# PixArt block on one core: banks of the maxima, place of a normalisation, and the order of loads in the start-up

## The chip, the cores and the metric

The kernel runs on one core of a Trainium2 chip. The metric is the device time of one execution in microseconds (us); three runs of the kernel before gave 813.94, 815.04 and 817.46 us, so its median is 815.04 us. A separate execution was profiled.

Engines: PE is TensorE (matrix products; PEld is its weight load, which runs ahead of it), DVE is VectorE, ACT is ScalarE, POOL is GpSimd, SP issues transfers (DMA). [...]

## What is computed

```python
x_norm = modulate(_ln(x), shift_a, scale_a)
q, k, v = split(x_norm @ W_qkv + b_qkv)           # 16 heads of 16
x = x + gate_a * ((softmax(q @ k.T * scale) @ v) @ W_proj + b_proj)
q_c = _ln(x) @ W_qc + b_qc;  k_c, v_c = split(_ln(context) @ W_kvc + b_kvc)
x = x + (softmax(q_c @ k_c.T * scale) @ v_c) @ W_cproj + b_cproj
h = gelu(modulate(_ln(x), shift_m, scale_m) @ W_mlp1 + b_mlp1) @ W_mlp2 + b_mlp2
x = x + gate_m * h
```

There are 16 batches of 256 tokens and 256 channels, in fp32. Shift, scale and gate come from `silu(cond_1024) @ W_mod + b_mod`.

## The kernel before, in words

**Units.** The work is 32 attention units: a self-attention (s) and a cross-attention (c) for each batch. Their order is s0 s1 s2 s3, then s4 c0 s5 c1 ... s15 c11, then c12 to c15. So from unit 4 to unit 27 the even units are s and the odd ones c. The MLP of all batches follows; some of its first steps lie in the last units.

**Beats.** One unit takes eight beats (`beat(n, k)`, line 944, k = 0 to 7; n is the unit whose softmax is being worked on, and n = -1 is a run of eight beats ahead of unit 0). A beat opens with `visit(n, k)` (line 929):

- `s_tile` (line 589) computes a tile of scores for the *next* unit, n+1, tokens in rows: four matmuls `s<-big` into the two banks of the PSUM tile `sp` (named s in the profile). One DVE instruction (`TENSOR_REDUCE mx<-s`, 128x1024) then takes the row maxima of both banks. The next beat's four matmuls may start only when it has ended, since they write the same two banks.
- `t_part` (line 624) computes the scores of the *current* unit with keys in rows, into the two banks of `st`; ACT takes their exponential (`pt<-st`). The maxima have become a row of the query tile before that.

After the visit a beat has pieces of other units: "lanes" (24 matmuls that run the projections of two units side by side), a transposition, or the product of exponentials and values, `av_part` (line 654, tile o).

**Around the change.** In beats 0 and 4 PE runs, after the visit, `m_part` (line 614, a transposition of the maxima, tile psm) and two `av_part` (32 matmuls into one bank, tile o). In beat 2, `turn(1)` of the previous unit (line 535) transposes the second half of its attention output into a bank (tile psA), and, where unit n+3 is s, its normalised x is transposed into another bank (psT_s), with the high part of the split by ACT (xTh_s) and the low part by DVE (xTl_s, 128x256 twice, in beat 3). `norm(1)` (line 542) of the previous unit reads psA on DVE: a reciprocal (rc) and a product (A). Before, it stands in beat 3 behind xTl_s. In beat 6, `turn(0)` transposes the first half for the current unit; if unit n+3 is c, a second transposition (psT_q) stands in that beat too.

**PSUM banks.** `sp` and `st` own two banks each. The other four are two tags of two banks: LONG ("gen", the lanes) and SHORT ("tr": psm, o, psT, psA and others). A SHORT tile gets the bank of the two that comes free first; it waits until the last reader of the tile before is done.

**Order.** Every engine runs its instructions in the order in which they are written (`InOrder`, line 40). The start-up is written as a list of words in `E_` (line 55). `PRE` is the list ahead of the first beat, `SL` the words behind a beat (n, k). Words that matter here: `ld2`, `ld3`, `ld4` load x of units 2 to 4 (SP); `one0` to `one2` write rows of ones into the three key tiles (SP); `z..` are the memsets of these tiles (POOL); `L2a L2b L2c` are the layernorm of unit 2 (statistics and variance on DVE, then power and application on POOL); `T2t T2h T2l` its transposition, high part (ACT) and low part (DVE), `T2p` the low part by ACT and POOL; `K2a K2m` its key projection (12 matmuls); `V0`, `V1` the value projections of units 0 and 1; `M0` an `m_part`; `b5`, `c4`, `d3` and so on are filler matmuls (4, 5, 3 ...) into sp, st or a SHORT bank; `vone` writes ones on POOL; `rest` takes the next step of `setup_rest` (line 221): first the loads for the attention's gate and bias rows (four weight or modulation tiles and bias rows; issued by ACT's queue before), then three small products ps_ga, ps_pb, ps_cb with DVE behind them, then three weight loads, then splits of weights on POOL.

Of the kernel before, what the change touches and what calls it, by code (L numbers as in the profile page):

```python
# [21 lines left out]
def pixart_block(  # L22
# [8 lines left out]
    B, N, H = x.shape  # L31
# [20 lines left out]
                return tc.keep_in_program_order(i) if self.on else i  # L52
            return issue

    E_ = {'M': ((-17, -12, -10, -1, 1), (0, 3, 4, 7, 9), (8, 11, 13, 15)), 'CUT': 8, 'LN': {'s': 'pool', 'c': 'pool', 'q': 'pool'}, 'ON': (1, 1, 1), 'L0': -16, 'L1': 1, 'S0': -7, 'A0': 0, 'T0': 1, 'H': (7, 11, 14, 15), 'S1': 5, 'A1': 7, 'L2': 9, 'T1': 9, 'S2': 32, 'AP': 23, 'DV': (0, 1), 'HP': (1, 0), 'BZ': {}, 'AV': {1: [(1, 2), (1, 3)], 9: [(0, 0), (0, 1)]}, 'AHEAD': (0, 0, 0, 0, 0, 2), 'W1P': [(-9, 1), (-8, 1), (-7, 1), (-6, 1), (-5, 1), (-5, 5), (-4, 1), (-4, 3), (-4, 5), (-3, 1), (-3, 3), (-3, 5), (-2, 1)], 'W2P': [(-4, 7), (-3, 0), (-3, 4), (-3, 6), (-3, 7), (-2, 2), (-2, 4), (-2, 6), (-1, 0), (-1, 1)], 'XP': 1, 'IL': 1, 'MF': 0, 'SH': 4, 'RAMP': 1, 'HA': 1, 'MP': 16, 'W': (7, 1, 0, 0), 'PRE': 'z0qp z0kp load silu b12 brow L0a turn L0b b4 L0d scale T0t sc1 hik lok T0h T0l b4 shift b4 hiq L1a L1b bk loq K0a K0b K0x0 K0x1 K0y0p K0y1p L1d T1t K0l T1h K0l0 K0l1 Q0a Q0m bq Q0h Q0x0 Q0y0p Q0x1 Q0y1p T1l Q0l Q0l0 Q0l1 ld2 z1kp z1qp K1a K1b hiv lov Q1a Q1b K1x0 K1x1 K1y0 K1y1 K1l K1l0 K1l1 Q1x0 Q1x1 Q1y0 Q1y1 Q1l Q1l0 Q1l1 V0a V0b bv b5 rest vone ld3 z2kp z2qp', 'SL': {(-1, 0): 'one0 c4', (-1, 1): 'ld4 L2a V1a', (-1, 2): 'L2b L2c V1b', (-1, 3): 'rest one1', (-1,4): 'M0 rest', (-1, 5): 'T2t T2h T2l rest', (-1, 6): 'L3a K2a c1', (-1, 7): 'K2m L3b L3p L3c c3 one2 rest', (0, 0): 'd4', (0, 1): 'rest', (0, 2): 'd3', (0, 4): 'rest', (1, 0): 'rest', (1, 2): 'rest', (1, 4): 'rest', (30, 0): 'd3', (30, 1): 'd2', (30, 2): 'd3', (30, 5): 'd3', (31, 1): 'd2'}}

    PE = InOrder(nc.tensor, True)
    ACT, DVE, POOL, SP = (InOrder(e, True) for e in (nc.scalar, nc.vector, nc.gpsimd, nc.sync))
# [162 lines left out]
    def setup_rest():  # L221
        gb = work.tile([B, 2, 2, H], F32, tag="pt", name="gb", bufs=5)
        gA, bb = gb[:, 0], gb[:, 1]
        bc = const.tile([1, H], F32, name="bc")
        wg, wp = stage(W_mod, 2 * H, "wga", "g", 3, q=ACT), stage(W_proj, 0, "wp_f", "g", 3, q=ACT)
        ACT.dma_start(bb[:, 0], b_mod[2 * H:3 * H].partition_broadcast(B))
        ACT.dma_start(bb[:, 1], b_proj.partition_broadcast(B))
        ACT.dma_start(bc, b_cproj.partition_broadcast(1))
        wcp = stage(W_cproj, 0, "wcp_f", "x1", 5, q=ACT)
        yield  # L230
        pst = ps_gen("ps_ga")
        for k in range(KC):
            PE.matmul(pst[:B, :H], sT[:, k], wg[:, k], start=(k == 0), stop=(k == KC - 1))
        DVE.tensor_tensor(gA[:, 0], pst[:B, :H], bb[:, 0], ALU.add)
        yield
        pst = ps_gen("ps_pb")
        for k in range(KC):
            PE.matmul(pst[:B, :H], bqkv[:, 4 + k], wp[:, k], start=(k == 0), stop=(k == KC - 1))
        DVE.tensor_tensor(gA[:, 1], pst[:B, :H], bb[:, 1], ALU.add)
        DVE.tensor_tensor(gA[:, 1], gA[:, 1], gA[:, 0], ALU.mult)  # L240
        SP.dma_start(gd[:, 0:2], gA)
# [12 lines left out]
        yield  # L254
        split(Wkc[0], Wkc[1], wkc)
        yield
        split(Wqc[0], Wqc[1], wqc)
        yield
        split(Wvc[0], Wvc[1], wvc)
        yield  # L260
        split(Wcp[0], Wcp[1], wcp)
# [324 lines left out]

    turn_of_s = [0]

    def s_tile(u, g, par, t, bank=None):


        alone = bank is None
        if alone:
            turn_of_s[0] ^= 1
            bank = turn_of_s[0]
        for j in range(2):
            PE.matmul(sp[:, bank, j * N:(j + 1) * N],
                      u.q[par * 64:par * 64 + 63, 2 * g + j, t * P:(t + 1) * P],
                      u.k[par * 64:par * 64 + 63, 2 * g + j, :], start=True, stop=True)
            if j == 0:  # L600
                yield
        if u.mx is None:
            u.mx = work.tile([P, 2, 2, 4, NT], F32, tag="mx", name=f"mx_{u.n}", bufs=3)
        mx = u.mx.rearrange("p f r a t -> p r f a t")
        a = slice(2 * (g % 2), 2 * (g % 2) + 2)
        if alone:
            DVE.tensor_reduce(mx[:, par, g // 2, a, t], sp[:, bank].rearrange("p (j n) -> p j n", j=2),
                              AX.X, ALU.max)
        elif bank == 1:
            DVE.tensor_reduce(mx[:, :, g // 2, a, t], sp.rearrange("p r (j n) -> p r j n", j=2),  # L610
                              AX.X, ALU.max)
        yield

# [63 lines left out]
    for n, (kind, b) in enumerate(seq):  # L677
        u = Box()
# [247 lines left out]
    def unit(n):  # L926
        return units[n] if 0 <= n < nu else None

    def visit(n, k):


        v, e = unit(n + 1), k
        s = []
        if v:
            s = [s_tile(v, e // 2, par, e % 2, par) for par in range(2)]
        if n < 0:
            in_turn(*s)
            return
        t = [t_part(units[n], k, par) for par in range(2)]
        in_turn(*s)  # L940
        in_turn(*t)
        later.append(lambda: exp(units[n], k))

    def beat(n, k):
        if n < 0:
            visit(n, k)
            return
        cur, prev, nxt = unit(n), unit(n - 1), unit(n + 1)
        q2, q3, q4 = (v if v and v.n >= m else None
# [20 lines left out]
            q2.Q.send_high()  # L970
        if k == 6 and q2:
            q2.V.keep()
        visit(n, k)
        if k == 0:
            if cur:
                m_part(cur, 1)
# [21 lines left out]
        elif k == 2:  # L998
# [3 lines left out]
            if q3T:  # L1002
                q3T.T[0].turn()
                q3T.T[0].high()
            if p2 and p2.hurry:
                p2.add()
        elif k == 3:
            exps()
            if q3T and q3T.kind == "s":
                q3T.T[0].low()  # L1010
            if prev:
                p1.norm(1)
            run(lanes(q2 and q2.V, q2 and q2.Q))
            if q3T and q3T.kind == "c":
                q3T.T[0].low()
        elif k == 4:
            if nxt:
                m_part(nxt, 0)
            exps()
            if cur:  # L1020
                av_part(cur, 0)
                av_part(cur, 1)
            if prev:
                p1.aT.turn()
                p1.aT.high()
            if q2:
                q2.Q.low()
                q2.Q.send_low()
            if p3:
                p3.store()  # L1030
            if late:
                for f in lx.ln[1].steps:
                    f()
            if ls and not late:
                ls.ln[0].steps[0]()
                ls.ln[0].steps[1](False)
        elif k == 5:
# [12 lines left out]
            v = unit(n + 5)  # L1050
            if v and v.kind == "c":
                load(v)
        elif k == 6:
            exps()
            if cur:
                cur.post.begin()
                cur.post.turn(0)
            if lx:
                lx.T[1].turn()
                lx.T[1].high()  # L1060
            if early:
                early.ln[1].steps[1]()
                early.ln[1].steps[2]()
            if prev and whole:
                p1.proj(0)
                p1.proj(1)
        elif k == 7:
            exps()
            run(lanes(None if whole else p1, q3 and q3.K))
            if prev and whole:  # L1070
                p1.end()
                p1.add()
                p1.store()
            if cur:
                cur.post.norm(0)
            if lx:
                lx.T[1].low()
# [97 lines left out]
```

## Time and profile before

| | |
|---|---|
| three runs | 813.94, 815.04, 817.46 us |
| the profiled execution | 815.38 us, of which the span from the first to the last instruction is 813.6 us |
| granted PE clock | 1.000 |
| PE busy, 100 to 500 us | 96.3 to 97.6 of each 100 us |
| DVE busy, 100 to 500 us | 81.8 to 83.8 of each 100 us |
| ACT busy, 100 to 500 us | 80.9 to 83.0 of each 100 us |
| POOL busy, 100 to 500 us | 54.3 to 59.9 of each 100 us |
| first score tile (beat 0 ahead of unit 0) | PE at 25.01 us |
| first beat of unit 0 | PE at 40.52 us |
| last product o | PEld at 617.6 us |

How to read the rows of the timeline: start in us, duration in us, engine, line, operation, tile written, tiles read, shapes, count; in square brackets the time for which the engine sat idle before it, and what ended that. Almost everything has line 51, which records every call, so rows are told apart by tile.

### The profile page before, as it was taken

The page shows a single profiled execution, that of the slowest core. Times are in us where ns is not written, and L with a number is a line of the kernel's source. Part 1 is how long each engine was busy: PE and PEld are TensorE (multiplying, and loading weights), DVE is VectorE, ACT ScalarE, POOL GpSimd, SP SyncE. Part 2 cuts the span into 40 slices and gives each one's busy share as a digit, 9 for nine tenths or more (in the row PEclk, how much of TensorE's full clock was granted, in tenths as well). Part 3 has the DMA queues.
Part 4 walks back from the last instruction along what each step waited for, and adds up shares of the span by engine and source line. Part 5 has one row for each costly group of instructions (what it writes and reads, how often), then busy time and mean ns, then how long its engine had stood idle before and what let it go on. Part 6 is the DMA issues. An engine that isn't in the chain of part 4 may idle for free.

```text
span 813.6 us, 23717 instructions
## 1 busy us (share of the span) xinstructions
PE 780.9 (96%) x9461; PEld 658.9 (81%) x9461; DVE 597.9 (73%) x1050; ACT 585.2 (72%) x1022; POOL 464.6 (57%) x404
## 2 busy tenths in 40 slices
PE   9899999999999999999999999999889999999997
PEld 8687877777787877877778788777668999999997
DVE  4787878788888878878887888776663566566562
ACT  3277877878787888878788788877656665666663
POOL 5555737475563647546364767554436666666653
PEclk9999999999999999999999999999999999999999
DMA  4753444335353444534444454534311313212211
GB/s 147 190 156 104 131 117 122 102 110 151 90 143 107 132 119 111 152 90 137 112 133 120 139 151 118 147 106 128 96 41 41 91 41 78 79 43 75 79 40 53
DMA packets 89938, 87.88 MB, mean 108 GB/s; under 512 B 9506, under 2 KB 85572, under 8 KB 89828
## 3 DMA queue, kind: packets, MB, share of 16 engines
q1 hardware_dynamic: 88482, 84.76, 37.3%
q8 instruction: 75, 1.23, 0.7%
q10 hardware_dynamic: 1154, 1.08, 0.5%
q0 software_dynamic: 192, 0.52, 0.2%
q14 instruction: 35, 0.29, 0.1%
HBM read 26.97 MB, written 8.46 MB: 44 GB/s over the span
## 4 chain that ended last, share of the span: by engine, by line
PE 69%; DVE 16%; issue 5%; POOL 4%; DMA 1%; ACT 0%; SPq 0%; POOLq 0%
PE s L51 15%; PE o L51 13%; DVE mx L51 12%; PE ph L51 11%; PE st L51 9%; PE ps_q L51 3%; PE ps_kc L51 3%; PE ps_k L51 3%; PE ps_P_s L51 2%; PE ps_qc L51 2%; PE ps_v_s L51 1%; PE ps_P_c L51 1%; DVE xTl_s L51 1%; PE psm L51 1%; PE psT_m L51 1%
## 5 line engine op out<-in xcount | busy, mean ns | idle before, releaser
L51 DVE TENSOR_REDUCE mx<-s 128x4 f32<-128x1024 f32 x256 | 313.3, 1224 | 103.2 <-PE s L51 98.1
L51 ACT ACTIVATE pt<-st 128x1024 f32<-128x1024 f32 x256 | 261.2, 1020 | 46.8 <-PE st L51 39.7
L51 PE MATMUL s<-big 63*128 63x256 f32 x1024 | 121.4, 309 | 15.8 <-DVE mx L51 13.5
L51 PE MATMUL o<-pt,v 128*32 128x256 f32 x2048 | 123.8, 382 | 3.1 <-DVE A_s L51 3.1
L51 PEld LDWEIGHTS s<-big 63*128 63x128 f32 x1024 | 80.5, 185 | 52.3 <-DVE mx L51 32.3
L51 POOL TENSOR_TENSOR hl<-hf,hh 128x512 fp32r<-128x512 f32 x64 | 89.0, 1399 | 55.5 <-ACT hh L51 54.4
L51 PE MATMUL st<-big 64*128 64x256 f32 x1024 | 107.1, 281 | 1.8 <-ACT pt L51 1.8
L51 PEld LDWEIGHTS o<-pt,v 128*32 128x32 f32 x2048 | 60.0, 109 | 45.0 <-DVE A_s L51 5.7
L51 PEld LDWEIGHTS st<-big 64*128 64x128 f32 x1024 | 82.0, 186 | 3.6 <-ACT pt L51 2.2
L51 ACT ACTIVATE hf<-ph,bT 128x256 f32<-128x256 f32 x120 | 50.6, 475 | 28.1 <-PE ph L51 28.1
L51 ACT COPY oT<-o 128x512 f32<-128x512 f32 x63 | 37.0, 587 | 46.0 <-PE o L51 46.0
L51 ACT ACTIVATE hh<-ph,bT 128x256 fp32r<-128x256 f32 x120 | 50.5, 471 | 24.6 <-PE s L51 12.8
L51 POOL TENSOR_TENSOR xTl_as<-y_as,xTh_as 128x512 fp32r<-128x512 f32 x16 | 20.4, 1272 | 62.9 <-ACT y_as L51 62.9
L51 POOL TENSOR_TENSOR xTl_c<-y_c,xTh_c 128x512 fp32r<-128x512 f32 x16 | 20.7, 1292 | 61.3 <-PE s L51 52.8
L51 PE MATMUL ph<-wqch,wself 128*128 128x256 f32 x256 | 51.8, 285 | 0.0
L51 PE MATMUL ph<-wkch,wself 128*128 128x256 f32 x256 | 51.7, 285 | 0.0
L51 POOL TENSOR_TENSOR xTl_ac<-y_ac,xTh_ac 128x512 fp32r<-128x512 f32 x16 | 20.5, 1279 | 53.0 <-ACT y_ac L51 49.1
L51 PE MATMUL s<-big,hh 128*128 128x256 f32 x256 | 47.4, 282 | 0.0
L51 PE MATMUL st<-big,hh 128*128 128x256 f32 x256 | 47.2, 281 | 0.0
L51 DVE TENSOR_SCALAR xn_m<-x,mv_m,rs_m 128x256 f32<-128x256 f32 x32 | 38.2, 1233 | 10.8 <-POOL rs_m L51 10.8
L51 PEld LDWEIGHTS ph<-wqch,wself 128*128 128x128 f32 x256 | 42.0, 191 | 0.4 <-issue 0.4
L51 PEld LDWEIGHTS ph<-wkch,wself 128*128 128x128 f32 x256 | 41.9, 191 | 0.4
(221 smaller groups left out, 2375.1 us busy)
## 6 DMA issues: line engine op xcount, KB each, us to landing
big<-h_kc SPq DMA_DIRECT2D x64, 128.0 KB
big<-h_qc SPq DMA_DIRECT2D x64, 128.0 KB
big<-h_k SPq DMA_DIRECT2D x62, 128.0 KB
big<-h_q SPq DMA_DIRECT2D x62, 128.0 KB
big<-l_k SPq DMA_DIRECT2D x32, 128.0 KB
big<-l_q SPq DMA_DIRECT2D x32, 128.0 KB
c<-in_ctx_dram SPq DMA_DIRECT2D x16, 256.0 KB
g<-gd SPq DMA_DIRECT2D x16, 256.0 KB
```

Source lines behind the costliest of these rows:

```text
L51: i = f(*a, **k)
```

## The change

Four things are changed. In the eight beats ahead of unit 0 the score tiles go to `st` and `sp` in turn (k even: st, k odd: sp). In "light" beats (k = 6, unit n+3 not c, n from 4 to 27, which leaves n = 5, 7, ..., 23) the two halves of a score tile go to bank 0 of sp and to a SHORT bank, each with a DVE maximum of its own (128x512). `norm(1)` moves from beat 3 to beat 2. The words of the start-up are reordered: the first step of `rest` stands right behind `load` and is issued by SP, with x of unit 2 and `one0` behind it; the layernorm of unit 2 stands ahead of the first beat; its transposition stands in beat 1 with its low part on POOL; fillers are dropped or changed.

```diff
-'PRE': 'z0qp z0kp load silu ... Q0l Q0l0 Q0l1 ld2 z1kp z1qp K1a ... Q1l Q1l0 Q1l1 V0a V0b bv b5 rest vone ld3 z2kp z2qp'
+'PRE': 'z0qp z0kp load rest ld2 one0 silu ... Q0l Q0l0 Q0l1 z1kp z1qp K1a ... Q1l Q1l0 Q1l1 L2a L2b L2c V0a V0b bv b5 ld3'
-'SL': {(-1, 0): 'one0 c4', (-1, 1): 'ld4 L2a V1a', (-1, 2): 'L2b L2c V1b', (-1, 3): 'rest one1', (-1,4): 'M0 rest',
-  (-1, 5): 'T2t T2h T2l rest', (-1, 6): 'L3a K2a c1', (-1, 7): 'K2m L3b L3p L3c c3 one2 rest', (0, 0): 'd4', ...
+'SL': {(-1, 0): 'V1a', (-1, 1): 'T2t T2h T2p vone z2kp z2qp', (-1, 2): 'V1b', (-1, 3): 'rest', (-1,4): 'M0 rest one1 ld4',
+  (-1, 5): 'K2a L3a', (-1, 6): 'K2m L3b L3p L3c', (-1, 7): 'd3 one2 rest', (0, 0): 'd6 rest', ...
@@ setup_rest
-        wg, wp = stage(W_mod, 2 * H, "wga", "g", 3, q=ACT), stage(W_proj, 0, "wp_f", "g", 3, q=ACT)
-        ACT.dma_start(bb[:, 0], b_mod[2 * H:3 * H].partition_broadcast(B))
...
+        wg, wp = stage(W_mod, 2 * H, "wga", "g", 3), stage(W_proj, 0, "wp_f", "g", 3)
+        SP.dma_start(bb[:, 0], b_mod[2 * H:3 * H].partition_broadcast(B))
...
@@ s_tile
-    def s_tile(u, g, par, t, bank=None):
+    def s_tile(u, g, par, t, bank=None, home=sp):
+        apart = isinstance(home, tuple)
         for j in range(2):
-            PE.matmul(sp[:, bank, j * N:(j + 1) * N],
+            PE.matmul((home[bank] if apart else home[:, bank])[:, j * N:(j + 1) * N],
...
-        if alone:
-            DVE.tensor_reduce(mx[:, par, g // 2, a, t], sp[:, bank].rearrange("p (j n) -> p j n", j=2),
+        if alone or apart:
+            src = home[bank] if apart else sp[:, bank]
+            DVE.tensor_reduce(mx[:, par, g // 2, a, t], src.rearrange("p (j n) -> p j n", j=2),
                               AX.X, ALU.max)
         elif bank == 1:
-            DVE.tensor_reduce(mx[:, :, g // 2, a, t], sp.rearrange("p r (j n) -> p r j n", j=2),
+            DVE.tensor_reduce(mx[:, :, g // 2, a, t], home.rearrange("p r (j n) -> p r j n", j=2),
@@ beat
         if n < 0:
-            visit(n, k)
+            visit(n, k, (st, sp)[k % 2])
...
-        visit(n, k)
+        light = k == 6 and nxt and 3 < n < nu - 4 and not lx
+        visit(n, k, (sp[:, 0], ps_gen("s1", SHORT)) if light else sp)
@@ beat, k == 2
+            if prev:
+                p1.norm(1)
             if p2 and p2.hurry:
                 p2.add()
@@ beat, k == 3
-            if prev:
-                p1.norm(1)
             run(lanes(q2 and q2.V, q2 and q2.Q))
```

`visit` hands its new argument `home` to `s_tile`.

More of the change, by code (lines that the diff above doesn't have):

```diff
@@ L53, in __getattr__ @@
             return issue
-    E_ = {'M': ((-17, -12, -10, -1, 1), (0, 3, 4, 7, 9), (8, 11, 13, 15)), 'CUT': 8, 'LN': {'s': 'pool', 'c': 'pool', 'q': 'pool'}, 'ON': (1, 1, 1), 'L0': -16, 'L1': 1, 'S0': -7, 'A0': 0, 'T0': 1, 'H': (7, 11, 14, 15), 'S1': 5, 'A1': 7, 'L2': 9, 'T1': 9, 'S2': 32, 'AP': 23, 'DV': (0, 1), 'HP': (1, 0), 'BZ': {}, 'AV': {1: [(1, 2), (1, 3)], 9: [(0, 0), (0, 1)]}, 'AHEAD': (0, 0, 0, 0, 0, 2), 'W1P': [(-9, 1), (-8, 1), (-7, 1), (-6, 1), (-5, 1), (-5, 5), (-4, 1), (-4, 3), (-4, 5), (-3, 1), (-3, 3), (-3, 5), (-2, 1)], 'W2P': [(-4, 7), (-3, 0), (-3, 4), (-3, 6), (-3, 7), (-2, 2), (-2, 4), (-2, 6), (-1, 0), (-1, 1)], 'XP': 1, 'IL': 1, 'MF': 0, 'SH': 4, 'RAMP': 1, 'HA': 1, 'MP': 16, 'W': (7, 1, 0, 0), 'PRE': 'z0qp z0kp load silu b12 brow L0a turn L0b b4 L0d scale T0t sc1 hik lok T0h T0l b4 shift b4 hiq L1a L1b bk loq K0a K0b K0x0 K0x1 K0y0p K0y1p L1d T1t K0l T1h K0l0 K0l1 Q0a Q0m bq Q0h Q0x0 Q0y0p Q0x1 Q0y1p T1l Q0l Q0l0 Q0l1 ld2 z1kp z1qp K1a K1b hiv lov Q1a Q1b K1x0 K1x1 K1y0 K1y1 K1l K1l0 K1l1 Q1x0 Q1x1 Q1y0 Q1y1 Q1l Q1l0 Q1l1 V0a V0b bv b5 rest vone ld3 z2kp z2qp', 'SL': {(-1, 0): 'one0 c4', (-1, 1): 'ld4 L2a V1a', (-1, 2): 'L2b L2c V1b', (-1, 3): 'rest one1', (-1,4): 'M0 rest', (-1, 5): 'T2t T2h T2l rest', (-1, 6): 'L3a K2a c1', (-1, 7): 'K2m L3b L3p L3c c3 one2 rest', (0, 0): 'd4', (0, 1): 'rest', (0, 2): 'd3', (0, 4): 'rest', (1, 0): 'rest', (1, 2): 'rest', (1, 4): 'rest', (30, 0): 'd3', (30, 1): 'd2', (30, 2): 'd3', (30, 5): 'd3', (31, 1): 'd2'}}
@@ new lines, in pixart_block @@
+    E_ = {'M': ((-17, -12, -10, -1, 1), (0, 3, 4, 7, 9), (8, 11, 13, 15)), 'CUT': 8, 'LN': {'s': 'pool', 'c': 'pool', 'q': 'pool'}, 'ON': (1, 1, 1), 'L0': -16, 'L1': 1, 'S0': -7, 'A0': 0, 'T0': 1, 'H': (7, 11, 14, 15), 'S1': 5, 'A1': 7, 'L2': 9, 'T1': 9, 'S2': 32, 'AP': 23, 'DV': (0, 1), 'HP': (1, 0), 'BZ': {}, 'AV': {1: [(1, 2), (1, 3)], 9: [(0, 0), (0, 1)]}, 'AHEAD': (0, 0, 0, 0, 0, 2), 'W1P': [(-9, 1), (-8, 1), (-7, 1), (-6, 1), (-5, 1), (-5, 5), (-4, 1), (-4, 3), (-4, 5), (-3, 1), (-3, 3), (-3, 5), (-2, 1)], 'W2P': [(-4, 7), (-3, 0), (-3, 4), (-3, 6), (-3, 7), (-2, 2), (-2, 4), (-2, 6), (-1, 0), (-1, 1)], 'XP': 1, 'IL': 1, 'MF': 0, 'SH': 4, 'RAMP': 1, 'HA': 1, 'MP': 16, 'W': (7, 1, 0, 0), 'PRE': 'z0qp z0kp load rest ld2 one0 silu b12 brow L0a turn L0b b4 L0d scale T0t sc1 hik lok T0h T0l b4 shift b4 hiq L1a L1b bk loq K0a K0b K0x0 K0x1 K0y0p K0y1p L1d T1t K0l T1h K0l0 K0l1 Q0a Q0m bq Q0h Q0x0 Q0y0p Q0x1 Q0y1p T1l Q0l Q0l0 Q0l1 z1kp z1qp K1a K1b hiv lov Q1a Q1b K1x0 K1x1 K1y0 K1y1 K1l K1l0 K1l1 Q1x0 Q1x1 Q1y0 Q1y1 Q1l Q1l0 Q1l1 L2a L2b L2c V0a V0b bv b5 ld3', 'SL': {(-1, 0): 'V1a', (-1, 1): 'T2t T2h T2p vone z2kp z2qp', (-1, 2): 'V1b', (-1, 3): 'rest', (-1,4): 'M0 rest one1 ld4', (-1, 5): 'K2a L3a', (-1, 6): 'K2m L3b L3p L3c', (-1, 7): 'd3 one2 rest', (0, 0): 'd6 rest', (0, 1): 'rest', (0, 2): 'd3', (0, 4): 'rest', (1, 0): 'rest', (1, 2): 'rest', (1, 4): 'rest', (30, 0): 'd3', (30, 1): 'd2', (30, 2): 'd3', (30, 5): 'd3', (31, 1): 'd2'}}
@@ L224, in setup_rest @@
         bc = const.tile([1, H], F32, name="bc")
-        wg, wp = stage(W_mod, 2 * H, "wga", "g", 3, q=ACT), stage(W_proj, 0, "wp_f", "g", 3, q=ACT)
-        ACT.dma_start(bb[:, 0], b_mod[2 * H:3 * H].partition_broadcast(B))
-        ACT.dma_start(bb[:, 1], b_proj.partition_broadcast(B))
-        ACT.dma_start(bc, b_cproj.partition_broadcast(1))
-        wcp = stage(W_cproj, 0, "wcp_f", "x1", 5, q=ACT)
+        wg, wp = stage(W_mod, 2 * H, "wga", "g", 3), stage(W_proj, 0, "wp_f", "g", 3)
+        SP.dma_start(bb[:, 0], b_mod[2 * H:3 * H].partition_broadcast(B))
+        SP.dma_start(bb[:, 1], b_proj.partition_broadcast(B))
+        SP.dma_start(bc, b_cproj.partition_broadcast(1))
+        wcp = stage(W_cproj, 0, "wcp_f", "x1", 5)
         yield
@@ L927, in unit, with visit @@
         return units[n] if 0 <= n < nu else None
-    def visit(n, k):
+    def visit(n, k, home=sp):
         v, e = unit(n + 1), k
@@ L934, in visit @@
         if v:
-            s = [s_tile(v, e // 2, par, e % 2, par) for par in range(2)]
+            s = [s_tile(v, e // 2, par, e % 2, par, home) for par in range(2)]
         if n < 0:
```

## The prediction

> **What bounds the kernel now.** I read the chain of work that ended last first, by engine:
>
> ```profile
> PE 69%; DVE 16%; issue 5%; POOL 4%; DMA 1%; ACT 0%; SPq 0%; POOLq 0%
> ```
>
> PE carries the path, and DVE's 16% of 813.6 us (130 us) are places where PE stands and waits for DVE. The list of waits says where (total us, times, longest):
>
> ```profile
> PEld s L51 <- DVE mx L51: 32.3, 70, 1.3
> ...
> PEld o L51 <- DVE A_s L51: 5.7, 12, 0.5
> ```
>
> So 32.3 us of idle weight load lie ahead of a score tile that waits for the maxima of the tile before, and 5.7 us ahead of a product o that waits for the normalised A. The change works on both. The timeline then gives the size of each. From 60 to 500 us it repeats every two units (35.2 us: o at 209.18 and again at 244.48), so one pair speaks for all.
>
> **Normalisation a beat sooner.** First an odd unit: DVE in beats 3 and 4, PE's weight load in beat 4; then the same loads in an even unit.
>
> ```profile
> 241.80 1.23 DVE L51 TENSOR_REDUCE mx<-s 128x4 f32<-128x1024 f32 x1 [0.60 <-PE s L51]
> 242.94 0.87 DVE L51 SCALAR_TENSOR_TENSOR xTl_s<-psT_s,sc,xTh_s 128x256 fp32r<-128x256 f32 x2
> 243.72 0.25 DVE L51 RECIPROCAL rc_s<-psA_s 128x16 f32<-128x16 f32 x1
> 244.00 0.42 DVE L51 TENSOR_TENSOR A_s<-psA_s,rc_s 128x256 f32<-128x256 f32 x1
> ```
>
> ```profile
> 243.36 0.33 PEld L51 LDWEIGHTS st<-big 64*128 64x128 f32 x4
> 243.92 0.09 PEld L51 LDWEIGHTS psm<-ident,mx 128*16 128x16 f32 x1 [0.23 <-PE st L51]
> 244.48 1.45 PEld L51 LDWEIGHTS o<-pt,v 128*32 128x32 f32 x32 [0.47 <-DVE A_s L51]
> ```
>
> ```profile
> 261.16 0.33 PEld L51 LDWEIGHTS st<-big 64*128 64x128 f32 x4
> 261.63 0.09 PEld L51 LDWEIGHTS psm<-ident,mx 128*16 128x16 f32 x1
> 261.84 1.45 PEld L51 LDWEIGHTS o<-pt,v 128*32 128x32 f32 x32
> ```
>
> Psm and o need the two SHORT banks that psA and psT_s hold. In the odd unit psm takes psT_s's when xTl_s ends (243.81), and o must wait for A (244.42). In the even unit nothing waits: psm follows st by 0.47 us, o follows psm by 0.21. With the pair in beat 2, psA's bank is free two microseconds before psm, and o takes psT_s's bank. In the written-out order of the changed kernel, psm indeed no longer waits for DVE, and o waits for xTl_s. Then psm starts at 243.36 + 0.47 = 243.83 and o at 244.04 instead of 244.48: 0.44 us. What is late next is xTl_s: 243.81 and a hand-over of some 0.1, so 0.12 before o needs it. All twelve cases (units 1, 3, ..., 23) show the same 0.23 and 0.47, so 12 x 0.44 = **5.3 us**. Upper end: psm right at the end of st's loads (243.69), 0.56 x 12 = 6.7. Lower end: psm still behind xTl_s and o 0.21 behind it, 0.35 x 12 = 4.2.
>
> The pair is not free, it is hidden. Between two maxima DVE has, in beat 2, an idle 0.60 us (the bracket of 241.80; the same 0.60 stands at 259.60 in the even unit). The pair takes 0.28 to the next start and 0.34 more, 0.62 in all, against 0.69 from where the maximum of beat 2 lets go (239.97 + 1.14) to 241.80. It reads psA, whose transposition ends at 240.76 (PE, 240.10 + 0.66), before DVE is free at 241.11. Queued behind it on DVE is the maximum of beat 3, which ends at 243.03; the score tile that waits for it loads at 243.13. So there is 0.1 us to spare, in each of 31 units. Without that cover the price is up to 0.62 x 31 = 19 us.
>
> Does the 0.44 reach the end? Behind o comes beat 5. ACT idled 1.01 us there until o ended, DVE idled 1.14 until the score tile came, so both move with PE. The transfers of unit n+2's queries do not: SP issues the last at 248.06 to 249.34, bytes move until about 250.7 (the DMA view), and the tile that reads them loads at 252.7. Two microseconds remain for 0.6 us of shift.
>
> **Light beats.** Beat 6 of the odd unit, PE's loads, then DVE and ACT:
>
> ```profile
> 249.51 0.42 PEld L51 LDWEIGHTS psA_c<-ident,oT 128*128 128x128 f32 x4
> 250.66 0.30 PEld L51 LDWEIGHTS s<-big 63*128 63x128 f32 x4 [0.73 <-DVE mx L51]
> 250.89 0.31 PEld L51 LDWEIGHTS st<-big 64*128 64x128 f32 x4
> ```
>
> ```profile
> 249.39 1.23 DVE L51 TENSOR_REDUCE mx<-s 128x4 f32<-128x1024 f32 x1
> ```
>
> ```profile
> 249.68 1.02 ACT L51 ACTIVATE pt<-st 128x1024 f32<-128x1024 f32 x1
> ```
>
> PE stands for 0.73 us until the maximum lets the next tile in. Split, the first half frees bank 0 sooner, and bank 1 was not used at all. No row shows a 128x512 maximum. Between the 128x256 product from PSUM (A, 0.42) and the 128x1024 maximum (1.22) lie 1.05 ns per element, so I estimate 0.69 us: the tile may load at 249.39 + 0.69 + 0.04 = 250.12, 0.54 sooner. But the loads behind it, st, wait for the exponential of beat 6, which ends at 250.70, and it cannot move: ACT is busy without a gap from 248.70. So st goes from 250.89 to 250.74, and the gain is 0.15, not 0.54. Ten light beats: **1.5 us** (0 to 2; 5.4 if ACT could follow). DVE pays one more start: two halves at 0.61 to the next against 1.14, 0.08 us, ahead of an idle 0.24, so nothing. [...]
>
> The SHORT bank makes two new waits. The half tile takes the bank that ACT's copy oT left (beat 4, long done). PsA_c now waits for ACT's y_as, which ends at 249.28 against a load at 249.51: 0.2 us to spare; queued behind psA on PE is the next score tile.
>
> **Four banks ahead of unit 0.** Weight loads of score tiles:
>
> ```profile
> 25.01 0.30 PEld L51 LDWEIGHTS s<-big 63*128 63x128 f32 x4
> 26.83 0.30 PEld L51 LDWEIGHTS s<-big 63*128 63x128 f32 x4 [0.42 <-DVE mx L51]
> ...
> 40.52 0.30 PEld L51 LDWEIGHTS s<-big 63*128 63x128 f32 x4
> ```
>
> Each beat is a tile, then its maximum, then the next: 1.83 us at least, and 15.5 us for eight. With four banks PE runs a beat ahead, and DVE's sum counts. The walk: the statistics of unit 2 (0.74 + 0.30 + 0.17) go into DVE's idle 0.90 ahead of 23.91; POOL's power (0.71) and application (2.44) then end at about 27.45. The transposition T2t waits for them on PE with beat 2's tile queued behind: tiles at 25.0, 26.2 and 28.1, maxima at 25.55, 26.7 and 28.55. From there DVE has six maxima (6 x 1.14), three gate rows (3 x 0.35) and unit 3's statistics (0.68 + 0.42): 9.0 us, and 0.2 for two hand-overs, to 37.8. PE's own sum in that stretch (tiles 6 x 0.44, V1 0.8, three small products 3.0, K2 1.5, psm 0.2, three fillers 0.8) ends at about 37.0. So unit 0 starts at 37.8 instead of 40.52: 2.7 us. In its first beat six fillers replace four (1.06 x 6/4 = 1.59 us) and start 0.78 us into it: beat 1 opens at 40.2 instead of 42.35. **2.2 us**; ends 2.9 (no stall at T2t) and 1.0 (application and gate rows each half a microsecond later than walked).
>
> What moves in the queues costs nothing in this walk. SP: six loads, x of unit 2 and one0 (0.39 to 0.61 us an issue) fill 4.6 to about 9 us; SP then idled until 14.20. Their bytes (4 x 256 KB and rows) follow the first loads, in slices of 1.75 us:
>
> ```profile
> GB/s 0 269 250 296 252 2 9 0 23 232 220 255 260 282 263 283 176 273 174 155 153 24 9 276 326 150 116 49 44 189 76 153 261 116 139 94 135 20 103 197
> ```
>
> At 250 to 290 GB/s they land by 13 us, in the empty slices, and leave the crowd of 20 to 30 us. POOL: the memsets (1.48 and 3.57 us) move behind xTl of unit 2 (31.1) and end near 36.2; unit 3's application then ends at 40, and its transposition is due at 43. Behind one2 and cd (which waits for DVE's last gate row, 38.1) SP holds the key transfers of unit 2, issued at 40.72 before. The three late weight loads go from 39.17 to about 44; POOL's cast waits for them until 47 with a power (51.99 before) behind it.
>
> **Sum.** 2.2 + 5.3 + 1.5 = 9.0 us off the profiled execution's 815.38: 806.4. That execution lies 0.34 above the median of the runs, so I forecast **806.1**.
>
> **Rivals.**
> - *The start-up gives nothing* (chance 0.12): unit 2's key transfers behind cd, or the application on POOL, come as late as the beats they were to free. For it: SP's queue held four issues for 4.47 us at 25.66. Against: SP idles in every walked stretch. 815.04 - 6.8 = 808.3.
> - *The product o still waits* (0.13): the banks go out otherwise, or beat 5 waits for ACT's pt instead. For it: a released bank goes to whoever asks first. 815.04 - 3.7 = 811.3, no change.
> - *Light beats give it all* (0.10): ACT follows PE, 5.4 instead of 1.5: 802.2.
> - *Slower* (0.05): in beat 2 the pair begins late (psA or its hand-over) and pushes the maximum of beat 3. For it: 0.1 us to spare. Against: psA ends 0.35 before DVE is free. Every 0.1 beyond the spare costs 3.1 us in 31 units; from 0.3 beyond it the gain is gone, from 0.42 it is slower by over 0.5%; at 0.62 it is 815.04 - 9 + 19 = 825.
>
> My forecast has 0.60. Its terms' ends give 1.0 + 4.2 + 0 = 5.2 to 2.9 + 6.7 + 2 = 11.6 us, so 803.4 to 809.8; to the light rival below and a little above: 802.0 to 810.5. Half a per cent (4.1 us, to 811.0) is about what a measurement of this kernel can tell from no change. Faster by more: 0.60 + 0.12 + 0.10 = 0.82; within: 0.13; slower: 0.05.
>
> **What would show it.** In the profile after: no o waiting for A_s, and o some 0.25 behind psm in odd units; maxima of beat 3 still 1.83 behind those of beat 2; 128x512 maxima (20 of them) of about 0.69 us; ahead of st in beat 7 a wait for pt where the wait for mx was; unit 0's first tile near 37.8 us. I am wrong if the pair pushes beat 3, or if the time between two units' o does not fall from 35.2 to 34.6 us.

## The result, and the profile after

The changed kernel takes **809.5 us** (median of 8 executions, 806.9 to 811.7) against 815.2 us of the kernel before (8 executions): ratio 0.9927, 95% interval 0.9905 to 0.9949, faster by 5.7 us. The forecast was 806.1 us, range 802.0 to 810.5. Two more sets of the same kernel later gave 810.4 us (ratio 0.9932, 0.9912 to 0.9953) and 808.4 us (0.9909, 0.9893 to 0.9925). Over all 20 executions the mean is 809.5 us, over 61 of the kernel before 816.0 us: **6.5 us less**, plus or minus 0.9. The profiled execution of the changed kernel took 807.08 us, its span is 805.3 us: 8.3 us less than the profiled execution of before.

First the chain of work of the changed kernel, then its list of waits (total us, times, longest us).

```profile
PE 74%; DVE 11%; issue 5%; POOL 4%; ACT 4%; DMA 2%; SPq 0%; POOLq 0%; ACTq 0%
```

```profile
PEld s L51 <- DVE mx L51: 22.7, 62, 1.4
...
PEld st L51 <- ACT pt L51: 6.1, 12, 1.4
```

DVE's share of the path fell from 16% to 11%, ACT's rose from 0% to 4%. The score tiles wait 22.7 us for maxima instead of 32.3, no product o waits for A_s any more (that row is gone), and ten waits of st for ACT's exponential are new. Before, there were two of these, 2.2 us.

**Odd unit, beats 2 and 3 on DVE, then PE's weight loads of beat 4** (unit 11, the unit that the prediction showed):

```profile
235.95 1.21 DVE L51 TENSOR_REDUCE mx<-s 128x4 f32<-128x1024 f32 x1
237.09 0.24 DVE L51 RECIPROCAL rc_s<-psA_s 128x16 f32<-128x16 f32 x1
237.36 0.42 DVE L51 TENSOR_TENSOR A_s<-psA_s,rc_s 128x256 f32<-128x256 f32 x1
237.76 1.23 DVE L51 TENSOR_REDUCE mx<-s 128x4 f32<-128x1024 f32 x1
238.90 0.87 DVE L51 SCALAR_TENSOR_TENSOR xTl_s<-psT_s,sc,xTh_s 128x256 fp32r<-128x256 f32 x2
```

```profile
239.34 0.33 PEld L51 LDWEIGHTS st<-big 64*128 64x128 f32 x4
239.80 0.09 PEld L51 LDWEIGHTS psm<-ident,mx 128*16 128x16 f32 x1
240.01 1.45 PEld L51 LDWEIGHTS o<-pt,v 128*32 128x32 f32 x32
```

The pair rc, A fills the 0.60 us in which DVE idled. The maxima start 1.81 us apart (237.76 - 235.95), so beat 3 is not pushed. Psm and o stand 0.46 and 0.21 us behind the load ahead of them, as in even units before. From the o of beat 0 to the o of beat 4 an odd unit takes 8.39 us instead of 8.83.

**Light beat**, PE's loads from psA_c on, then DVE, then the group of the half maxima in the table of groups (busy us, mean ns):

```profile
245.05 0.42 PEld L51 LDWEIGHTS psA_c<-ident,oT 128*128 128x128 f32 x4
245.64 0.30 PEld L51 LDWEIGHTS s<-big 63*128 63x128 f32 x4 [0.17 <-DVE mx L51]
246.30 0.30 PEld L51 LDWEIGHTS st<-big 64*128 64x128 f32 x4 [0.36 <-ACT pt L51]
```

```profile
244.89 1.29 DVE L51 TENSOR_REDUCE mx<-s 128x2 f32<-128x512 f32 x2
```

```profile
L51 DVE TENSOR_REDUCE mx<-s 128x2 f32<-128x512 f32 x20 | 12.9, 686 | 0.0
```

The tile s no longer loses 0.73 us but 0.17; st behind it stands 0.36 us for pt. From the o of beat 4 to the o of the next beat 0 it is 8.83 us instead of 8.97. A half maximum takes 0.686 us; the estimate was 0.69.

**Start-up**, unit 0's first score tile and that of its beat 1:

```profile
37.68 0.47 PEld L51 LDWEIGHTS s<-big 63*128 63x128 f32 x4 [0.93 <-DVE mx L51]
...
40.09 0.30 PEld L51 LDWEIGHTS s<-big 63*128 63x128 f32 x4
```

They were forecast for 37.8 and 40.2. (The 0.93 in brackets is the wait for the maximum ahead of it, as the walk had it: DVE's sum sets the end.)

| start of o (PEld), us | before | after | gain |
|---|---|---|---|
| unit 0, beat 4 | 49.14 | 46.69 | 2.45 |
| unit 11, beat 4 | 244.48 | 240.01 | 4.47 |
| unit 23, beat 4 | 456.74 | 448.20 | 8.54 |
| last o of the attention | 616.26 | 607.87 | 8.39 |

### The profile page after: what moved, and what is told of

It reads as the page before. It is cut to its first block, busy times and chain, and to the rows that moved or that the text cites. A ratio compares the mean times of both kernels' runs of the same rounds, so it can differ in the third digit from the quotient of the medians.

```text
span 805.3 us, 23708 instructions
## 1 busy us (share of the span) xinstructions
PE 781.0 (97%) x9455; PEld 659.1 (82%) x9455; DVE 595.7 (74%) x1058; ACT 584.9 (73%) x1024; POOL 465.6 (58%) x405
## 4 chain that ended last, share of the span: by engine, by line
PE 74%; DVE 11%; issue 5%; POOL 4%; ACT 4%; DMA 2%; SPq 0%; POOLq 0%; ACTq 0%
PE s L51 15%; PE o L51 13%; PE ph L51 11%; PE st L51 11%; DVE mx L51 8%; PE ps_qc L51 3%; PE ps_kc L51 3%; PE ps_q L51 3%; PE ps_P_s L51 2%; ACT pt L51 2%; PE ps_v_s L51 2%; PE psm L51 1%; PE ps_v_c L51 1%; PE ps_k L51 1%; PE ps_P_c L51 1%
## 5 line engine op out<-in xcount | busy, mean ns | idle before, releaser
L51 DVE TENSOR_REDUCE mx<-s 128x4 f32<-128x1024 f32 (+1 forms) x262 | 309.0, 1182 | 95.7 <-PE s L51 92.8
L51 PEld LDWEIGHTS s<-big 63*128 63x128 f32 x1008 | 80.0, 185 | 43.8 <-DVE mx L51 22.7
L51 PE MATMUL st<-big 64*128 64x256 f32 (+1 forms) x1040 | 110.2, 284 | 3.6 <-ACT pt L51 3.6
L51 PEld LDWEIGHTS st<-big 64*128 64x128 f32 (+1 forms) x1040 | 83.2, 186 | 8.2 <-ACT pt L51 6.1
```

Of the source, the lines that this page charges most:

```text
L51: i = f(*a, **k)
```

## Theories

**Theory:** the three parts act as walked and add: a bank that comes free sooner (norm, 0.44 us in each of 12 odd units), a beat bounded by DVE's sum instead of tile, maximum, tile (start-up), a light beat limited by the exponential (0.15 us each). **Rivals:** the pair pushes the maximum of beat 3; the order of the loads, not the banks, carries the start-up; the finer maximum, not the separate bank, carries the light beat. And one question the profile left: its execution gained 8.3 us, the medians 5.7. Where are the rest?

Below, differences are those of means, with 1.96 standard errors behind "plus or minus"; for sets of four to six executions a 95% interval is up to a third wider. Those against the kernel before are taken within one comparison, those against the changed kernel use its 20 executions; the means of the kernel before differ by 0.4 us between the later comparisons.

## Experiments 1 to 4: the parts alone, and the whole again

`norm_only`: the kernel before, with

```diff
@@ beat, k == 2, behind q3T.T[0].high()
+            if prev:
+                p1.norm(1)
@@ beat, k == 3
-            if prev:
-                p1.norm(1)
```

> The kernel before with one edit: the pair rc, A of the second half goes from beat 3 to beat 2. Theory (o is freed by the bank, nothing else changes): o waits for A_s in none of units 1, 3, ..., 23, and starts 0.25 us behind psm as in even units; 12 x 0.44 = 5.3 us less, a median near 810 against 815.2. Rival (the pair pushes the maximum of beat 3): beat 3's maxima more than 1.83 us behind beat 2's and a gain under 2 us. Rival (the gain needs the light beats, since beat 6 or 7 swallows what beat 4 wins): o starts sooner in beat 4 but the time between two units' o stays 35.2 us, no gain.

811.65 us, ratio 0.9947 (0.9927 to 0.9967), 4.5 us less (plus or minus 1.5). In the profile o waits for A_s nowhere, and the 12 odd units take 8.39 us instead of 8.83 where nothing else disturbs them. The theory holds; both rivals fall. One thing was in no theory: in unit 30 the tile s waits longer for the maximum than the same tile before (0.68 instead of 0.21 us). Before, then in `norm_only`:

```profile
587.93 0.30 PEld L51 LDWEIGHTS s<-big 63*128 63x128 f32 x4 [0.21 <-DVE mx L51]
```

```profile
584.19 0.30 PEld L51 LDWEIGHTS s<-big 63*128 63x128 f32 x4 [0.68 <-DVE mx L51]
```

The stretch from o to o around it takes 10.83 us instead of 10.36, the one ahead of it 9.34 instead of 9.18, an earlier one 9.40 instead of 9.58 to 9.65 (five profiles with the pair in beat 3). So some 0.4 us of the 5.3 is given back in the last units.

The rows ahead of that tile suggest why. DVE casts a weight for the MLP there, POOL works on the cast weight and then on x, and DVE's statistics `st_m` of this x stand in its queue ahead of the maximum. Before, then in `norm_only`:

```profile
582.49 0.42 DVE L51 CAST big<-w 128x512 fp32r<-128x512 f32 x1
...
585.58 0.75 DVE L51 BATCH_NORM_STATS2 st_m<-x 128x6 f32<-128x256 f32 x2 [0.45 <-POOL x L51]
```

```profile
578.75 0.41 DVE L51 CAST big<-w 128x512 fp32r<-128x512 f32 x1
...
581.84 0.75 DVE L51 BATCH_NORM_STATS2 st_m<-x 128x6 f32<-128x256 f32 x2 [1.54 <-POOL x L51]
```

The pair now stands ahead of the cast. Counted from the o of beat 4, the cast, POOL's step (0.13 to 0.14 us behind the cast's end in both), the statistics and the score tile are each 0.46 us later than before. No run tested this.

`light_only`: the kernel before with the edits of `s_tile` and `visit`, and

```diff
+        light = k == 6 and nxt and 3 < n < nu - 4 and not lx
-        visit(n, k)
+        visit(n, k, (sp[:, 0], ps_gen("s1", SHORT)) if light else sp)
```

> The kernel before with the light beats alone (ten beats 6 with two half maxima, the second tile half in a SHORT bank). Theory (the exponential of beat 6 lets the next tile st in only 0.1 to 0.15 us sooner): 1.2 to 1.5 us less, a median near 813.8, and a wait for pt ahead of st in beat 7 of those ten units. Rival (PE gets all of the 0.54 us): 5.4 us less, 809.8. Rival (a start of DVE and a new bank wait eat it): 815 or above.

814.66 us, ratio 0.9985 (0.9974 to 0.9995), 1.4 us less (plus or minus 0.8). The waits of s for mx fall from 32.3 to 28.9 us, those of st for pt rise from 2.2 to 6.0: what PE does not wait for DVE, it waits for ACT. The theory holds.

`start_only`: the kernel before with the new `E_`, the loads on SP, and

```diff
-            visit(n, k)
+            visit(n, k, (st, sp)[k % 2])
```

> The kernel before with the start-up edits alone (order of the words, loads on SP, four banks ahead of unit 0). Theory (ahead of unit 0 DVE's sum counts instead of tile, maximum, tile): unit 0's first tile near 37.7 instead of 40.5 us, beat 1 at 40.1 instead of 42.3, and 2.2 us less at the end, a median near 813.0. Rival (unit 2's key transfers or its statistics come as late as the beats that they were to free): the first tile early, but the gain lost by unit 2's beats, 815.

812.89 us, ratio 0.9964 (0.9952 to 0.9977), 2.8 us less (plus or minus 0.8). From the first score tile to the o of unit 0 it takes 21.98 us (25.49 to 47.47), against 24.13 before (25.01 to 49.14) and 21.92 in the changed kernel. That is 2.2 us, and it stays to the end.

`all_again`: no edit.

> The changed kernel itself, on the same chip as the three parts. If the parts add, its gain is the sum of theirs, 5.3 + 1.3 + 2.2 = 8.8 us by the walk, 806.4. Its executions spread from 806.9 to 811.7 us, those of before from 813.9 to 817.5. Theory A: the spread is that of single transfers that come late, as one did in the profile of before; then parts and whole spread alike, and a profile above 810 us shows one or a few stalls of PE of some 1 us each behind a DMA. Theory B: with PE nearer to full the granted clock falls; then an execution above 810 us has the same order of waits and a clock under 1.00 over a long stretch, 0.004 of 805 us being 3.2 us.

810.37 us, 808.1 to 813.3. The parts sum to 8.7 us (plus or minus 1.9), the whole gives 6.5 (plus or minus 0.9) over its three sets. The difference is taken up at the end. The profiled execution of `all_again`, at 808.14 us, has transfers in PE's way that the prediction had cleared. PE's loads of beat 0 of unit 18, then SP's issues ahead of it:

```profile
352.41 0.18 PEld L51 LDWEIGHTS s<-big 63*128 63x128 f32 x1
352.95 0.29 PEld L51 LDWEIGHTS s<-big 63*128 63x128 f32 x3 [0.36 <-DMA big<-l_qc]
```

```profile
344.28 3.74 SPq L51 DMA_DIRECT2D big<-h_qc  x4
348.12 1.42 SPq L51 DMA_DIRECT2D big<-m  x2
349.66 1.29 SPq L51 DMA_DIRECT2D big<-l_qc  x2
```

SP's four issues of h_qc took 3.74 us; in the kernel before the same four took 2.48. (Not everywhere: in other units of the profile of before four such issues took 3.40 us, at 314.35, and 4.10, at 101.69.) The low part l_qc was issued until 350.95 and held the score tile that reads it until 352.95. The changed kernel reaches that tile sooner, so such lateness is no longer covered. Waits of score tiles for these transfers add up to 1.4 us here, 0.55 in the first profile of the changed kernel, 0.4 in that of before.

## Experiments 5 to 8: the cover, the banks, and two limits

`rs_pool`: the changed kernel, with

```diff
-            DVE.tensor_scalar(o.rs, o.mv[:, :, 1], EPS, None, ALU.add)
+            (POOL if name[0] == "c" else DVE).tensor_scalar(o.rs, o.mv[:, :, 1], EPS, None, ALU.add)
```

The reason lies in the profile of `light_only`, whose execution (816.34 us) was the longest of its set. DVE, then POOL, ahead of the maximum of beat 2 in unit 11 (all but the last two rs_c lie in odd units; the expectation below says even ones):

```profile
238.47 0.75 DVE L51 BATCH_NORM_STATS2 st_c<-c 128x6 f32<-128x256 f32 x2 [0.47 <-DMA c<-in_ctx_dram]
...
240.53 1.30 DVE L51 TENSOR_SCALAR rs_c<-mv_c 128x2 f32<-128x2 f32 x1
241.75 1.21 DVE L51 TENSOR_REDUCE mx<-s 128x4 f32<-128x1024 f32 x1
```

```profile
239.28 1.29 POOL L51 TENSOR_TENSOR x<-xg,t_s 128x512 f32<-128x512 f32 x1
240.53 1.29 POOL L51 TENSOR_TENSOR xg<-x,g 128x512 f32<-128x512 f32 x1
```

A context tile landed 0.47 us late, so DVE's tiny rs_c (two elements a partition) fell on the start of POOL's xg instead of the end of POOL's x. It lasted until xg was done: 1.30 us. The next score tile then stood 1.09 us for the maximum. In three profiles (`light_only` and the first two of the changed kernel) rs_c ends about 0.02 us behind the end of POOL's instruction in 39 of 48 cases; in the other nine POOL is idle and it takes 0.17 us. What holds rs_c until then no row shows.

What a long rs_c costs can be read from the first profile of the changed kernel. The stretch from o to o around it takes 8.38 to 8.40 us for each rs_c of 0.17 to 0.48 us in an odd unit, then 8.43 us at 0.63, 8.62 at 0.83 and 9.00 at 1.21. So only what goes beyond some 0.6 us is on the path, and an rs_c of 0.17 us costs nothing there.

> The changed kernel with one more edit: rs_c = var + eps of the context units (128x2, beat 1 of even units) on POOL instead of DVE. In the profiles so far rs_c lasts 0.17 us where POOL is idle and else ends 0.02 us behind the end of whatever POOL runs, up to 1.31 us; 16 of them take 8.1 us in the changed kernel's profile, 10.6 in that of the light beats alone. Theory C (DVE's rs_c is held by POOL's instruction, and what of it goes beyond some 0.55 us delays the maximum of beat 2, with it the next score tile): without it 1.1 us less against the changed kernel's profile and up to 3.6 less where the phase is bad, a median 1 to 2.5 us under that of the changed kernel (810.4 on this comparison's chip), and a narrower spread than its 5 us. Rival (the spread comes from transfers that land late): the same median within 0.7 us and the same spread. Rival (POOL's extra instruction, some 0.7 us, delays its own queue): slower.

808.28 us, ratio 0.9900 (0.9883 to 0.9916): 1.3 us under the changed kernel (plus or minus 1.5). No rs_c is on DVE any more. The size is what theory C said, and the rival "slower" does not fit; against the rival "same within 0.7 us" this run alone does not decide, and five executions (806.8 to 810.4) are too few to call the spread narrower. `before_rs` below decides whether rs_c costs time; what makes the spread is taken up under `all_third`.

`cover`: the changed kernel, with

```diff
             DVE.reciprocal(rc, pv[:, :, :, HD:HD + 1])
+            if hf == 1:
+                DVE.reciprocal(rc, pv[:, :, :, HD:HD + 1])
```

> The changed kernel with the reciprocal of beat 2 done twice: 0.28 us more of DVE between the maxima of beats 2 and 3, in 31 units. It prices the cover of the moved pair. Theory (the maximum of beat 3 ends 0.13 us before the next score tile is due, by the profile of the changed kernel: 238.90 + 0.07 against 239.10): 0.28 - 0.13 = 0.15 us in 31 units, 4.7 us slower than the changed kernel (3.5 to 6). Rival (a later slack soaks it up, PE's queue has work in between): within 1 us of the changed kernel. Rival (all of it on the path): 8.7 us slower.

812.50 us, ratio 0.9954 (0.9939 to 0.9970): 3.1 us over the changed kernel (plus or minus 1.2); the spans of the profiles differ by 3.9 to 5.1 (810.4 against 805.3, 806.4 and 806.5). PE's score tiles of beats 2 and 3 in unit 11:

```profile
238.76 0.30 PEld L51 LDWEIGHTS s<-big 63*128 63x128 f32 x4 [0.32 <-DVE mx L51]
...
240.81 0.30 PEld L51 LDWEIGHTS s<-big 63*128 63x128 f32 x4
```

They are 2.05 us apart; in the changed kernel 1.88 (237.22 to 239.10). So 0.17 us of the 0.28 comes through between these tiles in units 1 to 29, and 0.13 from o to o: the cover is some 0.1 us thick, as the prediction priced it for the rival "slower". Soaking up nearly all, and taking the whole 8.7, are both excluded; the mean came out a little under the theory. Of the 5.1 us between the spans of this profile and the first of the changed kernel, 1.04 are another matter (a lower clock in unit 30, see `all_third`).

`light_sp`: the changed kernel, with

```diff
-        visit(n, k, (sp[:, 0], ps_gen("s1", SHORT)) if light else sp)
+        visit(n, k, (sp[:, 0], sp[:, 1]) if light else sp)
```

> The changed kernel with both halves of a light beat in the two banks of sp, so two maxima of 128x512 but no bank that lies apart. Theory (the tile of beat 7 needs both banks, and its second half waits for the second maximum, which ends 0.07 us later than one whole maximum would): the gain of the light beats is lost and 0.07 x 10 with it, 1.5 to 2 us slower than the changed kernel. Rival (the finer maximum frees the first bank, and that is enough since st waits for pt anyway): the same as the changed kernel within 0.5 us.

820.63 us, ratio 1.0058 (1.0039 to 1.0077): 11.6 us over the changed kernel (plus or minus 1.7). Neither expectation had that. The trace shows the place: PE's loads of the light beat itself.

```profile
212.28 0.30 PEld L51 LDWEIGHTS s<-big 63*128 63x128 f32 x3
213.58 0.18 PEld L51 LDWEIGHTS s<-big 63*128 63x128 f32 x1 [1.00 <-DVE mx L51]
```

```profile
212.84 0.69 DVE L51 TENSOR_REDUCE mx<-s 128x2 f32<-128x512 f32 x1
```

Three of the four matmuls run, the fourth waits 1.00 us for the maximum of the *first* half (212.84 + 0.69 = 213.53). In the order of the program that maximum stands ahead of the fourth matmul, and both touch one PSUM tile, sp. The matmul is held until the maximum is done, although it writes the other bank, which the second matmul had been free to write. In the changed kernel the order is the same and the second half is a tile of its own: there all four load without a break (0.30 us for the four, at 245.64). The light beat's stretch from o to o takes 9.98 us instead of 8.83; ten of these are the 11.6 us. "Banks that lie apart" is thus not an ornament of the light beat: the second half must be a tile of its own.

`st_late`: the changed kernel, with `visit` leaving out `t_part` when `hold` is set, and

```diff
+        hold = k == 7 and nxt and 3 < n < nu - 4 and not lx
...
         elif k == 7:
+            steps = lanes(None if whole else p1, q3 and q3.K)
+            if hold:
+                run(steps, 4)
+                in_turn(*[t_part(units[n], k, par) for par in range(2)])
+                later.append(lambda: exp(units[n], k))
             exps()
-            run(lanes(None if whole else p1, q3 and q3.K))
+            run(steps)
```

> The changed kernel, and in beat 7 behind a light beat four steps of the running products are issued between the score tile s and the tile st, so that PE has work while the exponential of beat 6 ends. Theory (st of beat 7 is held by the chain st, exponential, st of one pair of banks; PE could work in that 0.36 us): the wait for pt ahead of st goes in those ten units, PE ends beat 7 earlier by 0.36, and the next score tile takes 0.15 to 0.2 of it before it waits for the maximum: 1.5 to 2 us less than the changed kernel. Rival (all 0.36 reach the end): 3.6 us less. Rival (the exponential of beat 7 comes later and ACT becomes late): no gain or slower.

808.79 us, ratio 0.9900 (0.9884 to 0.9915): 1.3 us under the changed kernel (plus or minus 1.3). The stretch from o to o with the light beat takes 8.67 us instead of 8.83. So 0.16 of the 0.36 us reaches the end of the stretch, as the theory had it: the next tile s starts 0.05 us behind the end of the maximum ahead of it, so it cannot come sooner. In four of the ten units that tile then stands 0.2 to 0.5 us for l_qc. The times alone (1.3 plus or minus 1.3) would hardly tell the gain from none.

## Experiments 9 to 12: which half of the start-up, rs_c in both kernels, both edits together

`words_only`: `start_only` without its one line of the banks, so all tiles ahead of unit 0 in sp.

> The kernel before with the start-up edits except the banks: loads on SP and the new order of the words, but the score tiles ahead of unit 0 all in sp. Theory (ahead of unit 0 the chain tile, maximum, tile sets the end unless the banks take turns): eight beats of at least 1.83 us from the first tile, 14.6 us, so unit 0's first tile no sooner than 17.5 us behind its first score tile less 0.9 us of slack in that chain, a gain of 0 to 0.9 us against before; the start-up edits together gave 2.9 us (ratio 0.9964). Rival (the loads and the order of the words give it, the banks nothing): 2.5 to 3 us less than before.

816.54 us, ratio 1.0005 (0.9995 to 1.0016): no gain. PE's score tiles of the first beats:

```profile
25.08 0.30 PEld L51 LDWEIGHTS s<-big 63*128 63x128 f32 x4
26.91 0.30 PEld L51 LDWEIGHTS s<-big 63*128 63x128 f32 x4 [0.62 <-DVE mx L51]
28.73 0.30 PEld L51 LDWEIGHTS s<-big 63*128 63x128 f32 x4 [0.78 <-DVE mx L51]
```

Tile, maximum, tile: 1.82 us a beat. The order of words and loads gives nothing alone; it takes the banks to gain. (The banks without the words were not run, so how much of the 2.8 us needs both is open.)

`before_rs`: the kernel before with the one line of `rs_pool`.

> The kernel before with rs_c on POOL, nothing else. If what rs_c loses behind POOL's instruction is there in both kernels alike (1.7 us beyond 0.55 us in the profile of before, 1.1 in that of the changed kernel): about 2 us less than before, as in the changed kernel (810.4 to 808.3). If the changed kernel is the one that loses by it, because its beats fall later against POOL's instructions: under 0.7 us here, and this explains why the three parts together give 2 to 3 us less than the sum of their own gains (4.3, 1.2 and 2.9).

814.12 us, ratio 0.9979 (0.9970 to 0.9989): 1.7 us less (plus or minus 0.6). So rs_c behind POOL's instruction costs real time, and it does so in the kernel before as well. With that, my explanation for the parts summing to more than the whole falls.

`both`: the changed kernel with the edits of `rs_pool` and `st_late`.

> The changed kernel with both edits that helped: rs_c on POOL, and four steps of products between s and st in beat 7 behind a light beat. By the profiles the second is worth 0.16 us in each of ten units (8.67 instead of 8.83 us from one o to the next), the first 1 to 2.5 us; if they add, 1.6 us less than rs_c on POOL alone: 806.7, ratio 0.988. If they do not (the earlier end of beat 7 only waits for DVE): the same as either, 808.3 to 808.8.

**806.42 us**, ratio 0.9878 (0.9864 to 0.9892): 3.3 us under the changed kernel (plus or minus 1.1), the best of all. The profile shows both gains side by side: the stretch with the light beat takes 8.67 us, and the one that took 9.00 with an rs_c of 1.21 us takes 8.39. 1.3 and 1.3 make 2.6, which 3.3 fits; the intervals are too wide to say more of the sum.

`all_third`: no edit.

> The changed kernel once more, for its spread: the two profiles so far were the quickest executions of their sets (807.1 and 808.1 of sets that reach 811.7 and 813.3). Median 809.5 to 810.5. Theory C and late transfers together (first tile 22.5 to 23.7 us by when the first weights land; rs_c behind POOL's instruction; a context tile that lands 0.3 to 0.6 us late): a profile near the median has 2 to 3 us more in exactly these places than the first one, and nothing elsewhere. Rival (something that the profiles have not shown, such as the clock): the difference lies in a stretch without any of them.

808.43 us, 806.9 to 810.8; its profiled execution took 808.33 us. Against the first profile (span 806.5 against 805.3): the first score tile at 25.39 instead of 24.77 us, waits for l_qc at 178.69 (0.28 us) and 510.51 (0.16), and stretches 0.2 to 0.5 us longer in places that differ from execution to execution. No execution above 810 us of the changed kernel was caught in a profile.

The clock, theory B of `all_again`, can be checked without one, as the mean granted PE clock of every execution is on record. Of the changed kernel's 20, the eight at 0.996 or 0.997 took 809.9 to 813.3 us, and the twelve at 0.998 to 1.000 took 806.9 to 811.0, ten of them under 809. The groups' means differ by 2.7 us. So most long executions had a lower clock, as theory B said, but not all: two above 810 us had 0.999 and 1.000. One profile caught a stretch of low clock, that of `cover` (mean 0.997). PE was busy for 0.49 us between 577.67 and 579.67; from 580.67 to 583.67 its granted clock was 0.50. The product o in it took PE 3.48 us, the o before it (at 570.95) 1.93. Its first loads:

```profile
580.67 0.20 PEld L51 LDWEIGHTS o<-pt,v 128*32 128x32 f32 x8 [0.20 <-issue]
581.10 0.20 PEld L51 LDWEIGHTS o<-pt,v 128*32 128x32 f32 x4 [0.23 <-issue]
```

That stretch from o to o took 11.87 us instead of 10.83. One such place would account for 1.0 of the 2.7 us; what else a long execution has on top stays open. That a fuller PE brings the clock down is not shown either: `rs_pool` and `both` are faster still, and their means are 0.9996 and 0.9990.

## Why the prediction was right, and where it was off

All three medians lie in the range. It was close: the ends of the terms alone reached 809.8 us, and 809.5 and 808.4 lie under that, 810.4 does not. The gain was forecast at 9.0 us and is 6.5 in the mean. The mechanisms held; these are the terms.

- **Start-up, 2.2 us.** Right, in its steps too: first tile 37.68 (37.8 forecast), beat 1 at 40.09 (40.2). Of the 2.45 us at the first o, 0.24 is not the change's: the first score tile came at 24.77 instead of 25.01 us. Over the ten profiles with the changed start-up words it comes between 24.77 and 25.91, over the four with the old ones between 24.95 and 25.56.
- **Norm, 5.3 us.** The size in the odd unit is right: from the load of st to that of o it is 0.43 to 0.46 us less, twelve times, 5.4 in all. Cover and order held; the price of the cover was confirmed by `cover`. What the walk did not have is the 0.4 us given back in the last units.
- **"Does the 0.44 reach the end?" Two microseconds remain for 0.6 us of shift.** This is the step that failed. I took the margin of the query transfers from one unit and used it for all. In `all_again` unit 18's tile stood 0.36 us for l_qc, and the profile of before already had issues of 3.4 and 4.1 us beside the 2.5 that I read. Lined up against before, five stretches from o to o are 0.06 to 0.15 us longer even in the best of four profiles (three of the changed kernel, one of `rs_pool`): 0.5 us in sum. Three of them, 0.3 us in sum, have the extra in beat 0's score tile, whose loads take 0.45 us or more instead of 0.3. That tile reads the new queries, so late transfers are the likely reason, but no wait is recorded in these rows. The other two, behind beat 4 of units 0 and 10, are as long in `start_only`; their cause is open.
- **Light beats, 1.5 us.** The mechanism is right (s freed, st held by pt). Each gives 0.13 to 0.15 us, but in the changed kernel only in seven of ten: 1.0 us. The reason I gave was half of it: ACT starts that exponential at 245.22, when its copy of v is out of the way, but st's matmuls of beat 6 end only at 245.12, and elsewhere an idle ACT starts 0.10 us behind them. Both limits meet, so by these rows taking the copy away would win next to nothing (no run shows it).
- **The price of the split.** Two halves take 1.29 us on DVE, one whole 1.22: 0.07 us more (the prediction had 0.08). Two of 0.686 make 1.37, and the second starts 0.08 us before the first ends. None of it was on the path.
- **The sum.** With these sizes, 2.2 + 5.4 - 0.4 - 0.5 + 1.0 = 7.7 us is my estimate of what an undisturbed execution gains; I had 9.0. The profiled pair shows 8.3: the execution of before that I summed against also had its first tile 0.24 us later, and by difference some 0.4 us more of late tiles and long rs_c. The mean over executions is 6.5 (plus or minus 0.9). That the parts alone sum to 8.7 (plus or minus 1.9) is hardly outside the intervals; its cause was not settled. The growing waits for query transfers would fit, but were seen only at 0.4 to 1.4 us. The clock goes the same way: its mean is 0.9982 over the changed kernel's executions, 0.9989 to 0.9992 over those of the three parts and 0.9991 over 53 of the kernel before. How much of the gap it makes is not shown.

The rivals: "start-up gives nothing", "o still waits" and "slower" are excluded by the profile; "light beats give it all" by the 0.36 us wait for pt.

## What to carry to other kernels

When a stall is taken away, ask of every transfer into that stretch how late it may be in *each* repetition, not in the one that was read: a margin is its smallest value. Before a tile is cut in two so that halves come free sooner, see to it that the halves are tiles of their own in the program's eyes; here, in one tile, the later writer waited 1.00 us for the earlier reader (`light_sp`). And when executions of one kernel differ by more than the effect, line up the same tile in several profiles: here it showed a two-element instruction that took up to 1.31 us.

## What was not expected of the hardware

- rs_c on DVE, 128x2, lasts 0.17 us beside an idle POOL and up to 1.31 us beside a busy one; it ends some 0.02 us behind POOL's instruction. With it on POOL the kernel before took 1.7 us less.
- Four issues of 128 KB by SP took 2.48 us in one execution and 3.74 in another, for the same unit.
- The first score tile starts 24.77 to 25.91 us into the span, 1.1 us apart, in profiles that have the same start-up words.
- The granted PE clock of a kernel on one core is not always 1: it was 0.50 for 3 us in the profile of `cover`, and the stretch with it took 1.04 us more.
